# Four state-space layers on one core: the lines layer's table of slots is rearranged

## The chip, the cores and the metric

The kernel runs on one core of a Trainium2 chip. Its time is the device time of one execution in microseconds (us); the median of three runs is 17365.62 us (17365.36 to 17379.11). The engines are TensorE (PE: matrix products), VectorE (DVE), ScalarE (ACT), GpSimd (POOL) and SyncE (SP), which here only issues DMA transfers. Each works through its own queue of instructions in order and waits on semaphores for the others.

## What is computed

Eight images of 48 x 48 pixels and 96 channels go through four layers, each with a group norm before it and a residual addition behind it. Layers 0 and 3 are two-dimensional selective scans over 2304 positions, layer 1 is a filtered two-layer perceptron, and layer 2, the "lines" layer, scans every row and every column of 48 pixels in both senses. Its core, for one direction:

```python
xz = x @ in_w
xi, z = jnp.split(xz, 2, axis=-1)
xi = jax.nn.silu(causal_conv4(xi) + conv_b)
dt_low, Bm, Cm = jnp.split(xi @ xproj_w, [6, 22], axis=-1)
dt = jax.nn.softplus(dt_low @ dt_w + dt_b)
h = exp(dt * A) * h + dt * xi * Bm        # 192 channels x 16 states, along the line
y = (sum(h * Cm) + D * xi) * jax.nn.silu(z) @ outp_w
```

The four directions are then projected with `out_w`, summed and added to x.

## The kernel before, in words

**Layers.** `ss2d` runs layers 0 and 3, `lines` runs layer 2. Layer 1 has no stage of its own: its work items ("guests", class `Guest`) are slipped in between the work of layer 0 and of the lines layer. A guest item is a few matmuls into a PSUM bank that is free at that moment, and in the next slot an ACT instruction that takes the result out (`settle`).

**Blocks, turns, slots.** `scans` is shared by all three scan layers. The work is cut into images (8), directions (4) and blocks of 10 rows, 480 columns (the fifth block of a direction has 8 rows, 384 columns): 160 blocks a layer. A block has 8 slots, one for each pair of channel half and group of four states (`ORDER`), and two slots make a turn; so turn 0 holds slots 0 and 1, turn 3 slots 6 and 7. A slot has three units of [128 x columns], a turn six, which three scan instructions on DVE (L335) take two by two. I number the scans of a block 0 to 11.

**What one turn needs.** For every unit, ACT makes exp(dt * A) into one of two PSUM tiles `da` (L327, two instructions for each scan, so exp of scan n+2 can start when scan n has ended). The product of step size, input and B, called `dbu`, is made a turn ahead (L303), by DVE or POOL as the table `ON_POOL_L2` says: {slot: units of three that POOL makes}. DVE takes B from PSUM, where ACT copies it first (`copy_b`, L284, one bank; slots 3 and 4 have the same B and share a copy); a slot that POOL makes whole has no copy. After a scan, POOL multiplies by C (`make_hc`, L341, three units), and PE sums the states (`reduce`, L361 and L363).

**Order within a turn t** (end of `scans`), which is the order of every queue: scan 3t; POOL's C product for the slot before; `dbu` of the next turn's first slot on DVE; exp; both `dbu` of the next turn on POOL; scan 3t+1; exp; copy of B and `dbu` of the next turn's second slot on DVE; PE's sums; then the `aside` of the even slot; POOL's C product; exp for the next turn; scan 3t+2; copy of B; the gate product (L935) in turns 0 and 2; and the `aside` of the odd slot.

**`aside(at)`** (L405 to L425) settles the guest of the slot before, issues the loads due in this slot (B and C by `LOAD_BC`, the step sizes by `LOAD_DD`), runs the preparation steps (`stage1`) of the blocks to come, then the project and add steps of the block behind (`done`), and lets in a guest. The preparation of a block starts two blocks early; steps numbered 8 to 10 fall into slots 0 to 2 of the block before it:

```python
return {3: conv(0), 4: conv(1), 6: s2s3, 7: s5, 8: s6, 9: s7, 10: s8}
```

`conv` is four matmuls (L870) into the bank "sb" or "sa"; `s2s3` a Silu on ACT (L879) and a matmul (L889, bank "sa"); `s5` copies the result out (L894) and starts the step-size matmuls (L900); `s6` is Softplus on ACT (L907); `s7` the z matmuls (L913), the product dt * xi on POOL (L503) and the stores of the step sizes to DRAM (`store_dd`, L489); `s8` the Silu of z (L922). Silu, Softplus and exp need different function tables on ACT, so each of these steps brings two table loads. The stored step sizes are loaded back, spread over the partitions, by `load_dd` (L256), half 0 and half 1 of the block apart, into three rotating buffers. `project` (L944, bank "sa") and `add` (L950 or L952, DVE, `x += result`) follow a finished block. Banks open to guests by slot:

```python
guest.banks = lambda slot, clear: {0: ["sa"], 2: ["sb"], 3: ["sa"], 6: ["sb"]}.get(slot, [])
```

`guest.rate = 0.42` adds credit each slot, and an item costs 1.0.

Of the kernel before, what the change touches and what calls it, by code (L numbers as in the profile page):

```python
# [29 lines left out]
NG = 8  # L30
ORDER = [(0, sg) for sg in range(4)] + [(1, sg) for sg in range(3, -1, -1)]
LOAD_BC = (1, 1, 6, 7)
LOAD_DD = (3, 5)
NBUF = 7
UP = 96
UG = 73
# [8 lines left out]
CH = 96  # L45

ON_POOL_SS = {2: 1, 3: 3, 5: 1, 6: 1, 7: 3}
ON_POOL_L2 = {3: 2, 5: 3, 6: 1, 7: 3}


DIRS_SS = [(False, False), (True, False), (False, True), (True, True)]
# [10 lines left out]
def rows(t, n):  # L62

    return t[:, :n].rearrange("p (r s) -> p r s", s=SEG)
# [37 lines left out]
def vss_stack_kernel(ctx: ExitStack, tc: tile.TileContext, i: dict, out: bass.AP):  # L102
# [120 lines left out]
    def scans(dirs, order, restart, on_pool, a, pools, ps, stage1, opening, done, side, tail, ahead=None, guest=None):  # L223
# [9 lines left out]


        ahead = ahead or iter(())
        blocks = [Block(job, k, blk, n == 0, n == len(BLKS) - 1, dirs[k][1])
                  for job in range(nb) for k in order
                  for n, blk in enumerate(range(len(BLKS))[::-1 if dirs[k][1] else 1])]
# [14 lines left out]
        def load_dd(b, half):  # L253

            t = pools["dd"].tile([P, 3 * 2 * WMAX], F32, tag="dd", name="dd")
            nc.sync.dma_start(t[:, :6 * b.m], b.dd[half].unsqueeze(1).to_broadcast([32, 4, 6 * b.m]))  # L256
            b.got[half] = t[:, :6 * b.m].rearrange("p (g t m) -> p g t m", g=3, t=2)

        def load_bc(t):

            b, slot = blocks[t // NG], t % NG
            sg = ORDER[slot][1]
            other = t - slot + NG - 1 - slot
            n = min(free, key=lambda n: free[n])
            free[n] = other
            r = bufs[n]
            rows4 = b.bcd[8 * sg:8 * sg + 8, :].rearrange("(s w) n -> s (w n)", w=2)
            nc.sync.dma_start(r[:, LEAD:LEAD + 2 * b.n], rows4.unsqueeze(0).to_broadcast([32, 4, 2 * b.n]))

            lo, hi = LEAD - b.at.start, LEAD + b.n  # L270
            bcs[t] = bcs[other] = r[:, lo:hi + b.at.start], r[:, hi:hi + b.n]
# [105 lines left out]
        def run(t):  # L377
            for step in steps.pop(t, []):
                step()
# [25 lines left out]
        def aside(at):  # L405

            nblk, slot = at // NG + 1, at % NG
            if guest:
                guest.settle()
            if nblk < len(blocks):  # L410
                for n, of in enumerate(LOAD_BC):
                    if of == slot:
                        load_bc(NG * nblk + n)
                if slot in LOAD_DD:
                    load_dd(blocks[nblk], LOAD_DD.index(slot))
            clear = next(beside, True)
            run(at)
            for step in later.pop(at, []):
                step()
            while tail:  # L420
                tail.pop(0)()
            if guest:
                guest.turn(slot, clear)

        for t, (b, q) in enumerate(turns):  # L425
            at, nblk = 2 * t, t // (NG // 2)
# [64 lines left out]
    def sizes(b, half):  # L491

        return [b.dds[:, half, n, b.at] for n in range(2)]

    def make_room(b, pools):
        b.room = pools["dds"].tile([DH, LEAD + 4 * WMAX], F32, tag="dds", name="dds")
        b.dds = b.room[:, LEAD:LEAD + 4 * b.m].rearrange("p (h t m) -> p h t m", h=2, t=2)
# [279 lines left out]
    def lines(xin, xout, guest):  # L777
# [22 lines left out]
        def shift(t, dy, dx):  # L800

            at = (pad + dy) * step + pad + dx
            return t[:, at:at + H * step].rearrange("p (h w) -> p h w", w=step)[:, :, :W]
# [52 lines left out]
        def stage1(b):  # L856
            n = b.n
            col, rev = dirs[b.k]
            got = {}

            def shifted(off):
                return shift(colwise if col else rowwise, 0, off)[:, b.r0:b.r0 + b.nr, :]

            def conv(half):
                def run():
                    got["u", half] = ps("sa" if half else "sb", 1)
                    for tap in range(4):
                        off = tap - 3 if not rev else 3 - tap
                        at = ((b.k * 4 + tap) * 2 + half) * DH
                        nc.tensor.matmul(got["u", half][:, :n], lhsT=wide("cw", at),  # L870
                                         rhs=shifted(off), start=(tap == 0), stop=(tap == 3))
                return run

            def s2():
                b.uball = ubs[(len(BLKS) * (NK * b.job + b.k) + (len(BLKS) - 1 - b.blk if rev else b.blk)) % 3]
                b.uball = b.uball.rearrange("p (h n) -> p h n", h=2)
                b.ub = b.uball[:DH]
                for half in range(2):
                    nc.scalar.activation(b.ub[:, half, :n], got["u", half][:DH, :n], AF.Silu,  # L879
                                         bias=w["l2_cb"][:, b.k, half:half + 1])  # L880

            def s2s3():
                s2()
                s3()

            def s3():
                got["p"] = ps("sa", 1)
                for half in range(2):
                    nc.tensor.matmul(got["p"][:, :n], lhsT=wide("xp", (2 * b.k + half) * NBC), rhs=b.uball[:, half, :n],  # L889
                                     start=(half == 0), stop=(half == 1))  # L890

            def s4():
                b.bcl = pools["bcl"]
                nc.scalar.copy(b.bcl[:NBC, :n], got["p"][:NBC, :n])  # L894

            def s5():
                s4()
                for half in range(2):
                    got[half] = ps("sb" if half else "sa", 1)
                    nc.tensor.matmul(got[half][:, :n], lhsT=wide("dtw", (2 * b.k + half) * DH), rhs=b.bcl[:, :n],  # L900
                                     start=True, stop=True)

            def s6():
                nc.sync.dma_start(b.bcd, b.bcl[:2 * NS, :n])
                make_room(b, pools)
                for half in range(2):
                    nc.scalar.activation(sizes(b, half)[0], got[half][:DH, :n], AF.Softplus,  # L907
                                         bias=w["l2_dtb"][:, b.k, half:half + 1])

            def s7():  # L910
                for half in range(2):
                    got["z", half] = ps("sb" if half else "sa", 1)
                    nc.tensor.matmul(got["z", half][:, :n], lhsT=wide("inz", (2 * b.k + half) * DH),  # L913
                                     rhs=shifted(0), start=True, stop=True)
                make_du(b, b.ub[:, :, :n].rearrange("p h (r s) -> p h r s", s=SEG))
                for half in range(2):
                    store_dd(b, half)

            def s8():
                b.zb = up.tile([DH, 2, BMAX], F32, tag="zb", name="zb")  # L920
                for half in range(2):
                    nc.scalar.activation(b.zb[:, half, :n], got["z", half][:DH, :n], AF.Silu)  # L922

            return {3: conv(0), 4: conv(1), 6: s2s3, 7: s5, 8: s6, 9: s7, 10: s8}

        def opening(b, half):
            return wide("diag", (2 * b.k + half) * DH), b.uball[:, half, :b.n]
# [3 lines left out]
        def done(b, half, y):  # L931
            n = b.n
            if half == 0:
                gated[b] = gp.tile([DH, 2, BMAX], F32, tag="gated", name="gated")
            nc.vector.tensor_mul(gated[b][:, half, :n], b.zb[:, half, :n], y[:DH, :n])  # L935
            if half == 0:
                return []
            got = {}

            def project():  # L940
                got["o"] = ps("sa", 1)
                t = gated.pop(b)
                for h in range(2):
                    nc.tensor.matmul(got["o"][:, :n], lhsT=wide("wo", (2 * b.k + h) * C, DH), rhs=t[:, h, :n], start=(h == 0), stop=(h == 1))  # L944

            def add():
                xv = seq(xs[b.job], dirs[b.k][0])[:, b.r0:b.r0 + b.nr, :]
                v = rows(got["o"][:C], n)
                if b.k == 0:
                    nc.vector.scalar_tensor_tensor(xv, v, w["l2_outb"], xv, ALU.add, ALU.add)  # L950
                else:
                    nc.vector.tensor_add(xv, xv, v)  # L952
                if b.k == NK - 1 and b.last:
                    nc.sync.dma_start(xout[b.job], xs[b.job])

            return [(1, project), (2, add)]

        def side(job):
            used = NG
# [21 lines left out]
                yield from front(job + 1, tail.append, wait())  # L981

        dirs = DIRS_L2
        guest.banks = lambda slot, clear: {0: ["sa"], 2: ["sb"], 3: ["sa"], 6: ["sb"]}.get(slot, [])
        guest.psum = lambda tag: ps(tag, 1)
        guest.rate = 0.42
        scans(dirs, range(NK), True, ON_POOL_L2, a, pools, ps, stage1, opening, done, side, tail, guest=guest)
        stack.close()

# [264 lines left out]
    guest = Guest(stack, x1, x2)  # L1254
# [98 lines left out]
```

## Time and profile before

| what | value |
|---|---|
| profiled execution, time / span | 17373.84 us / 17371.9 us |
| median of the runs | 17365.62 us |
| lines layer, first dbu to last add | 5899 to 11833 us |
| its images 1 to 7, from output to output | 759, 737, 761, 742, 736, 724, 704 us |
| busy over the whole span | PE 76%, DVE 91%, ACT 80%, POOL 88% |
| last guest result stored | 10045 us |
| granted TensorE clock | 0.843 |

A page of the profile gives busy time by engine and by group of instructions (line, engine, operation, tile written from tiles read, shape), with the idle time ahead of a group and what ended it. The list of waits gives for each pair of waiting group and releaser the total in us, the number of times and the longest. A timeline row is: start in us, duration in us, engine, line, operation, tiles, shape, how many instructions are merged in it, and in brackets the idle time before it with its releaser. The window rows give for a stretch its length and then, for PE, PEld (weight loads), DVE, ACT and POOL, the busy us and the number of instructions, then the granted clock, DMA share and GB/s.

### The profile page before, as it was taken

The numbers are of one execution on the slowest core, as the hardware profiler recorded it, in microseconds if no ns is written. First come the engines' busy times: TensorE is split into PE (matmuls) and PEld (weight loads), VectorE is DVE, ScalarE is ACT, GpSimd is POOL, SyncE is SP. The second block draws the span as 40 slices with busy tenths as digits, with TensorE's granted clock in tenths as the row PEclk, the third lists the DMA queues.
The fourth block names the chain that finished last, engine by engine and source line by source line (L and its number), as shares of the span: only waits on it lengthen the run. The fifth ranks groups of instructions, "written<-read, shape, count | busy, mean of one in ns | idle before, by whom it ended". The sixth has DMA issues, their size and how long they took to land.

```text
span 17371.9 us, 169003 instructions
## 1 busy us (share of the span) xinstructions
PE 13193.7 (76%) x53740; PEld 4744.7 (27%) x53740; DVE 15807.2 (91%) x9840; ACT 13897.8 (80%) x20972; POOL 15212.7 (88%) x8159
## 2 busy tenths in 40 slices
PE   6778788878787677777777777776777777777776
PEld 1223232323232333233233322221222222222221
DVE  7999999998899789899889999996999999999998
ACT  6888888878787688888888888886878878878876
POOL 7998888988889788888888888887999999999998
PEclk7888888888897888899889988887878878878877
DMA  4555555454545344444444444443455555555454
GB/s 141 178 174 169 176 168 179 167 183 165 173 169 181 130 149 165 149 157 154 156 155 149 159 158 155 150 155 128 171 173 176 174 174 175 174 169 179 169 176 144
DMA packets 887919, 2843.67 MB, mean 164 GB/s; under 512 B 353468, under 2 KB 421788, under 8 KB 760206
## 3 DMA queue, kind: packets, MB, share of 16 engines
q1 hardware_dynamic: 887022, 2832.85, 48.0%
q8 instruction: 423, 6.93, 0.2%
q14 instruction: 474, 3.88, 0.1%
HBM read 2384.40 MB, written 448.17 MB: 163 GB/s over the span
## 4 chain that ended last, share of the span: by engine, by line
ACT 22%; DVE 21%; POOL 19%; issue 14%; PE 13%; DMA 10%; SPq 1%; POOLq 0%; DVEq 0%; ACTq 0%
DVE dbu L335 14%; POOL dbu L341 12%; ACT ps_da L327 8%; DVE dbu L303 6%; POOL dbu L303 4%; DMA dd<-dds 4%; DMA dd<-dd 3%; ACT L327 3%; PE ps_y L361 2%; POOL dds L503 2%; ACT ps_b L284 1%; PE ps_sa L944 1%; PE ps_sa L889 1%; DMA bc<-bcd 1%; ACT L907 1%
## 5 line engine op out<-in xcount | busy, mean ns | idle before, releaser
L335 DVE TENSOR_TENSOR_SCAN dbu<-ps_da,dbu 128x968 f32<-128x968 f32 (+3 forms) x5760 | 11823.5, 2075 | 814.5 <-ACT ps_da L327 653.1
L341 POOL TENSOR_TENSOR dbu<-dbu,bc 128x1440 f32<-128x1440 f32 (+1 forms) x3840 | 10069.9, 2635 | 1775.7 <-DVE dbu L335 1715.3
L327 ACT ACTIVATE ps_da<-dd,w_l_a 128x484 f32<-128x484 f32 (+3 forms) x11520 | 7423.0, 649 | 2308.3 <-DVE dbu L335 2078.8
L361 PE MATMUL ps_y<-dbu,w_red 128*32 128x480 f32 (+1 forms) x23040 | 4206.5, 651 | 1588.0 <-POOL dbu L341 1554.0
L363 PE MATMUL ps_y<-dbu,w_red 128*32 128x480 f32 (+1 forms) x7680 | 4168.0, 651 | 0.0
L303 DVE TENSOR_TENSOR dbu<-dd,ps_b 128x962 f32<-128x962 f32 (+5 forms) x2880 | 3831.0, 1330 | 286.1 <-ACT ps_b L284 157.3
L303 POOL TENSOR_TENSOR dbu<-dd,bc 128x481 f32<-128x481 f32 (+5 forms) x2240 | 3913.5, 1762 | 22.5 <-DMA dd<-dd 18.2
L361 PEld LDWEIGHTS ps_y<-dbu,w_red 128*32 128x32 f32 x23040 | 724.9, 118 | 5000.1 <-POOL dbu L341 3338.6
L284 ACT COPY ps_b<-bc 128x482 f32<-128x482 f32 (+3 forms) x2720 | 1448.8, 533 | 227.1 <-DVE dbu L303 185.3
L578 PE MATMUL ps_side<-xpad,w_l_cw 128*128 128x480 f32 (+1 forms) x2880 | 1360.4, 611 | 46.4 <-ACT g_room L1179 16.3
L327 ACT ACT_TABLE_LOAD x993 | 1274.0, 1283 | 17.5
L707 PE MATMUL ps_s<-bcl,square 128*128 128x480 f32 (+1 forms) x1280 | 890.0, 786 | 324.1 <-ACT dds L711 169.5
L357 PE MATMUL ps_y<-big,eye 128*128 128x480 f32 (+1 forms) x960 | 745.0, 865 | 243.5 <-ACT big L758 238.9
L717 PE MATMUL ps_s<-big,square 128*128 128x480 f32 (+1 forms) x1280 | 844.9, 790 | 66.1 <-ACT g_room L1179 18.4
L503 POOL TENSOR_TENSOR dds<-dds,big 96x960 f32<-96x960 f32 (+1 forms) x320 | 706.7, 2209 | 144.9 <-ACT dds L735 144.6
L578 PEld LDWEIGHTS ps_side<-xpad,w_l_cw 128*128 128x128 f32 x2880 | 575.0, 210 | 815.0 <-issue 703.4
L889 PE MATMUL ps_sa<-ub,square 128*128 128x480 f32 (+1 forms) x640 | 411.7, 782 | 394.2 <-ACT ub L879 394.2
L363 PEld LDWEIGHTS ps_y<-dbu,w_red 128*32 128x32 f32 x7680 | 661.9, 118 | 0.0
L870 PE MATMUL ps_sb<-xpad,square 128*128 128x480 f32 (+1 forms) x1280 | 595.2, 611 | 84.7 <-ACT g_room L1179 32.7
L870 PE MATMUL ps_sa<-xpad,square 128*128 128x480 f32 (+1 forms) x1280 | 537.9, 561 | 0.0
L711 ACT ACTIVATE dds<-ps_s,w_l_dtb 96x480 f32<-96x480 f32 (+1 forms) x640 | 405.1, 633 | 124.6 <-DMA dd<-dds 82.9
L758 ACT COPY big<-ps_y 96x480 f32<-96x480 f32 (+1 forms) x640 | 471.6, 737 | 38.7 <-PE ps_y L363 37.4
(244 smaller groups left out, 12498.7 us busy)
## 6 DMA issues: line engine op xcount, KB each, us to landing
dd<-dd SPq DMA_DIRECT2D x512, 1452.0 KB
bc<-bcd SPq DMA_DIRECT2D x1536, 480.0 KB
dd<-dd SPq DMA_DIRECT2D x256, 1440.0 KB
dd<-dds SPq DMA_DIRECT2D x512, 363.0 KB
dd<-dd SPq DMA_DIRECT2D x128, 1164.0 KB
bc<-bcd SPq DMA_DIRECT2D x384, 384.0 KB
dd<-dds SPq DMA_DIRECT2D x256, 360.0 KB
dd<-dd SPq DMA_DIRECT2D x64, 1152.0 KB
```

Of the source, the lines that this page charges most:

```text
L284: nc.scalar.copy(bps[t][:, :bcs[t][0].shape[1]], bcs[t][0])
L303: engine.tensor_mul(o, du, by.unsqueeze(1).to_broadcast([P, hi - lo, by.shape[1]]))
L327: nc.scalar.activation(da[:, at:at + b.m], b.got[half][:, u % 3, 0, :], AF.Exp, scale=a[:, b.k, ci:ci + 1])
L335: nc.vector.tensor_tensor_scan(db, da, db, 0.0, ALU.mult, ALU.add)
L341: nc.gpsimd.tensor_mul(h, h, bcs.pop(2 * t + sub)[1].unsqueeze(1).to_broadcast([P, 3, n]))
L361: nc.tensor.matmul(y[32 * g:32 * g + 32, :n], lhsT=wc["red"][:, :32], rhs=hc[:, g, b.at], start=False, stop=(slot == 3))
L363: nc.tensor.matmul(y[DH:, :n], lhsT=wc["red"][:, 32:], rhs=hc[:, 2, b.at], start=False, stop=(slot == 3))
L503: nc.gpsimd.tensor_mul(du, dt, u)
L578: nc.tensor.matmul(pu[:, :n], lhsT=flat[:, at:at + P], rhs=xpad[:, r0 + dy:r0 + dy + nr, dx:dx + W], start=(tap == 0), stop=(tap == 8))
L707: nc.tensor.matmul(got["p"][:, :n], lhsT=wide("dtw", (2 * b.k + half) * DH), rhs=b.bcl[:, :n], start=True, stop=True)
L717: nc.tensor.matmul(got["p"][:, :n], lhsT=wide("xp", (2 * b.k + half) * NBC), rhs=uall[:, half], start=(half == 0), stop=(half == 1))
L870: nc.tensor.matmul(got["u", half][:, :n], lhsT=wide("cw", at), rhs=shifted(off), start=(tap == 0), stop=(tap == 3))
```

## The change

Only tables and slots of the lines layer change. The addition to x moves from two to three slots behind the finished block (slot 3 to slot 4); the two convolutions from slots 3 and 4 to 4 and 5; the load of step-size half 0 from slot 3 to slot 2; POOL makes `dbu` of slots 4, 6 and 7 whole, instead of two units of slot 3, slot 5 whole, one unit of slot 6 and slot 7 whole (nine units either way); and guests may enter in slots 0, 3 and 6 instead of 0, 2, 3 and 6. Layers 0 and 3 keep their tables.

```diff
-LOAD_DD = (3, 5)
+LOAD_DD_SS = (3, 5)
+LOAD_DD_L2 = (2, 5)
...
-ON_POOL_L2 = {3: 2, 5: 3, 6: 1, 7: 3}
+ON_POOL_L2 = {4: 3, 6: 3, 7: 3}
...
+        load_in = LOAD_DD_L2 if restart else LOAD_DD_SS
...
-                if slot in LOAD_DD:
-                    load_dd(blocks[nblk], LOAD_DD.index(slot))
+                if slot in load_in:
+                    load_dd(blocks[nblk], load_in.index(slot))
...
-            return {3: conv(0), 4: conv(1), 6: s2s3, 7: s5, 8: s6, 9: s7, 10: s8}
+            return {4: conv(0), 5: conv(1), 6: s2s3, 7: s5, 8: s6, 9: s7, 10: s8}
...
-            return [(1, project), (2, add)]
+            return [(1, project), (3, add)]
...
-        guest.banks = lambda slot, clear: {0: ["sa"], 2: ["sb"], 3: ["sa"], 6: ["sb"]}.get(slot, [])
+        guest.banks = lambda slot, clear: {0: ["sa"], 3: ["sb"], 6: ["sb"]}.get(slot, [])
```

## The prediction, made before the changed kernel ran

> **What bounds the kernel now.** Only the lines layer is touched, so I read the window rows of that stage first, then its list of waits, then one block as a timeline.
>
> ```profile
> 5900.00:11800.00 5900.00, 4506.11 (x18182) 1721.81 (x18182) 5345.67 (x3421) 4883.50 (x7125) 4893.75 (x2267) 0.87 0.44 154
> ```
>
> The third busy figure is DVE's: 5345.67 of 5900 us, 91%; ACT and POOL stand at 83%. DVE bounds the stage, and a change can win at most its 554 us of idle time. The waits say what ends it:
>
> ```profile
> DVE dbu L335 <- ACT ps_da L327: 275.0, 252, 3.3
> ...
> DVE x L952 <- PE ps_sa L944: 128.7, 105, 3.2
> ...
> DVE dbu L303 <- DMA dd<-dd: 93.8, 48, 34.3
> ...
> DVE x L950 <- PE ps_sa L944: 45.3, 35, 2.6
> ...
> SPq L256 <- DMA dd<-dds: 1696.6, 295, 9.0
> ```
>
> Numbering the scans of each block along DVE's timeline puts these waits in place. Scan 3 (the first of turn 1) waits for its exp in 158 of 160 blocks, 191 us; the add waits for its projection 141 times, 175 us; the first dbu of the next block, in turn 3, waits for step sizes 47 times, 59 us (the 34 us one is the start of the layer); scans 0 and 1 wait 28 and 38 us. The last row is on SP: the load of the step sizes waits for their own store. One block, DVE first:
>
> ```profile
> 8996.45 2.16 DVE L335 TENSOR_TENSOR_SCAN dbu<-ps_da,dbu 128x960 f32<-128x960 f32 x1 [1.64 <-ACT ps_da L327]
> 8998.52 1.63 DVE L303 TENSOR_TENSOR dbu<-dd,ps_b 128x1440 f32<-128x1440 f32 x1
> 9000.07 4.20 DVE L335 TENSOR_TENSOR_SCAN dbu<-ps_da,dbu 128x960 f32<-128x960 f32 x2
> 9004.87 0.71 DVE L950 SCALAR_TENSOR_TENSOR x<-ps_sa,w_l_outb,x 96x480 f32<-96x480 f32 x1 [0.60 <-PE ps_sa L944]
> ```
>
> ```profile
> 8998.64 1.36 ACT L327 ACTIVATE ps_da<-dd,w_l_a 128x480 f32<-128x480 f32 x2 [0.49 <-DVE dbu L335]
> 9000.02 1.28 ACT L922 ACT_TABLE_LOAD   x1
> ...
> 9002.36 1.28 ACT L327 ACT_TABLE_LOAD   x1
> 9003.65 1.36 ACT L327 ACTIVATE ps_da<-dd,w_l_a 128x480 f32<-128x480 f32 x2
> ```
>
> ```profile
> 8996.52 1.56 SPq L489 DMA_DIRECT2D dd<-dds  x2
> 9006.98 5.22 SPq L256 DMA_DIRECT2D dd<-dd  x2
> ```
>
> See two things. Scan 5 ends at 9004.27, but the exp for scan 6 ends at 9005.01: the add's wait covers ACT being 0.74 us late behind the Silu of z. And the load of step sizes leaves 10 us after the store; the dbu that needs it came at 9015.66 after a wait of 0.24, so it took 8.7 us.
>
> **POOL's units.** By shape, DVE makes 3, 2 and 1 units in 1630, 1126 and 628 ns, POOL 3, 2 and 1 in 2738, 1887 and 1036. DVE's block was 4 x 1630 + 1126 + 628 = 8274 ns, and becomes 5 x 1630 = 8150: 19 us less over the blocks. The weight is in where they go.
>
> Turn 0 gains: dbu of slot 3 is three units instead of one on DVE, 1.0 us more work (0.8 in short blocks) ahead of scan 3, which waits there for ACT in any case. Taking from each block's wait the smaller of wait and 1.0 gives 129 us over the 156 blocks whose rows I could follow.
>
> Turn 1 loses: dbu of slot 5 comes to DVE, so its copy of B (L284, 540 ns) now stands ahead of the Silu of z on ACT; before, slot 5 had no copy, and that of slot 6 stood behind the exp. There are five copies either way.
>
> Turn 2 puts slots 6 and 7 whole on POOL, two operations of 2.74 us in a row between C products. From the end of scan 1 POOL then has nine of 2.74 and the dt * xi product with its memset (2.02) up to the C product of slot 5, 26.6 us, and PE's sums behind it take 1.7. Scan 3 starts about 4.3 us after scan 1's end, so PE is free 24.0 us into turn 1. Behind those sums on PE stands L889, which ACT's Silu releases at 9.0 (to scan 6, next part) + 7.6 (turn 2: three scans, add, gate) + 7.0 (scan 9, dbu, copy, table load, two Silu) = 23.6. PE would be 0.4 us late; in the block above, where scan 3 waited long, not at all. The result goes by L894 to the exp of scan 1. In the 108 blocks with guests half have under 0.35 us of slack there; block by block a slip of 0.2, 0.4 or 1.0 us costs 8, 19 or 61 us. The 47 blocks without guests have 1 us of slack: nothing. I take 0.3 us, 13 us; it cannot gain, since PE waits for the Silu now. The dbu themselves are in time: slot 4 at 6, slots 6 and 7 at 14 and 17 us into turn 1, wanted at 9.0, 16.6 and 20.2.
>
> **Add and convolutions.** The projection stays in slot 2, so an add two scans later finds it done: 171 us of wait go (156 blocks). What is late next is the exp of scan 6. From the end of scan 3, ACT takes 6.40 us in the block above, plus 0.54 for the copy, 6.94; DVE has two scans and a dbu, 5.66. So 1.28 us of waiting in long blocks, and since ACT was 1.4 us late in short ones, 1.9 there: over all blocks 242 us, where add and scan 6 waited 177. This part costs 65 us. The add's own 0.7 to 0.9 us only moves. From below: were the copy hidden, this place would gain 17. The convolutions (2.85 us each) move behind the sums of turn 1 on PE; bank "sb" is settled in slot 4 ahead of the first, "sa" read by the add ahead of the second, and slot 6 reads them 4 us later. PE was idle 2.5 us ahead of L889 per block, so I count nothing beyond the slip above.
>
> **Step sizes.** In the queue order of the changed program the load moves past at most a guest transfer. In 124 of 156 blocks nothing stood between store and load, and it still left 9.6 us after the store: SP waits for the store, not for the slot. The two blocks where three or four guest transfers came between (16 us) and the others with such a neighbour waited about 16 us above the rest; from 0 to 16, I take 10.
>
> But the round trip is a loop: store to load 9.6, load to dbu 8.7, then 17.7 to the next store (four scans, three dbu, the C product and the dt * xi product). 36.0 us a block, beside a mean long block of 37.5. Whatever is won between store and dbu is only kept where the step sizes have landed. Sum so far: 129 - 65 + 19 = 83 us, 0.53 a block. In 46 blocks DVE already waits there, so all is lost; elsewhere the spare time (dbu less load less 8.65, 7.4 in short blocks) is under 0.43 us in a quarter of the long ones. Cutting each block's gain at its spare time leaves 51 us.
>
> Here the Trainium skill differs ("DMA: Bandwidth & Descriptors", section "Anatomy of one DMA — SWDGE (gpsimd) path"): about 2.0 us plus bytes over 436 GB/s. It is stated for another issuing engine; for the 360 KB store it would be 2.8 us, an estimate. Then loads would leave 6.8 us sooner, the loop would not bind, and the 83 would stand. The row has 9.6 us in nearly every block, so I take 51.
>
> **Guests.** At three places a block instead of 3.36 by credit, the last result is stored, by the order of SP's queue, about 12 blocks later. Long blocks with guests last 38.0 us, without 36.4. If an item costs, nothing changes; if a block with guests costs, 12 x 1.6 = 19 us. I take 12. One guest fewer between z and the convolutions frees PE, not DVE.
>
> **Sum.** 51 + 10 - 13 - 12 = 36 us off the profiled 17373.8. That execution is 8.2 us above the median of the runs, so the time is 17365.6 - 36 = 17330.
>
> **The rivals.** *Exchange without gain*, 20%: the loop of step sizes takes all; landing 1 us later than 8.65, as with bc loads and guests beside it in a dozen blocks, eats another 35, and 17360 is left. For it: the 1696 us of SP waits; against it: half of the blocks have 1 us to spare. That moving the load does nothing is in both.
>
> *POOL's row of four*, slower, 19%: in turn 2 the C products come so late that PE starts L889 1.5 us late, and `s5`, the exp and scan 1 follow in all guest blocks: 61 + 108 x 0.5 = 115 us, against 51 + 10 - 12 = 49 of other gain: 66 us slower, 17432; at 1.2 us (83) still 34 slower, 17400. It decides from a slip of about 0.85 us, where the 49 are gone. For it: POOL has no pause from scan 1 to there; against it: the count of its work gives 0.4.
>
> *More*, 20%: the copy of B falls into a pause of ACT and transfers land sooner once the order is quieter: without the copy the sum is 164 before the loop's cut and 82 after it, 92 with the ordering: 17274, and 17250 if the cut is a quarter smaller.
>
> *As summed*, 41%, own range 17305 to 17352.
>
> **Numbers.** About 0.2% (35 us) is what a measurement can tell from no change. Faster by more: the 20% and two thirds of 41%, 0.47; within: the rest and the exchange, 0.34; slower 0.19. For 8 in 10 the range goes from 17250 to 17405.
>
> **What would show it.** Right: the add's waits nearly gone; scan 3 waiting 0.2 to 0.4 us a block instead of 1.2; scan 6 waiting 1.3 to 1.9 us for ACT, about 240 us in all; dbu on step sizes above 59 us; store to load still 9.6. Wrong: scan 6 not waiting, scan 1 waiting over 100 us, or the load leaving sooner after its store.

## The result, and the profile after

Changed kernel: 17276.92 us, median of six runs (17266.99 to 17280.5); before, six runs, 17368.66. The ratio is 0.9944 (0.9931 to 0.9957): 92 us or 0.5% faster. The direction was forecast, the size was 36. The profiled execution has a span of 17274.2 us (17371.9 before), so the sums below are made against 97.7. The lines layer's images 1 to 7 now take 740, 728, 733, 727, 732, 723 and 699 us; the last guest is stored at 10395 instead of 10045 us; the granted clock over the span is 0.849.

The window row of the lines stage, after (stretch and length, then busy us of PE, PEld, DVE, ACT, POOL, then granted clock, DMA share, GB/s):

```profile
5900.00:11700.00 5800.00, 4406.68 (x18177) 1666.92 (x18177) 5333.69 (x3261) 4882.12 (x7124) 4868.65 (x2107) 0.89 0.45 157
```

DVE still bounds the stage: 5333.69 of 5800 us, 92%. Its list of waits, after:

```profile
DVE dbu L337 <- ACT ps_da L329: 347.2, 301, 3.3
DVE dbu L305 <- DMA dd<-dd: 113.4, 72, 35.1
```

Waits for `ps_sa` by the add have left the list but for one of 1.9 us; scans waiting for exp grew from 275 to 347 us, and `dbu` waiting for step sizes from 94 to 113 (35 of each is the start of the layer). SP's row for the load that waits for its store says that this round trip has not become shorter:

```profile
SPq L258 <- DMA dd<-dds: 1763.7, 314, 8.9
```

One block on DVE, after:

```profile
9068.22 1.65 DVE L305 TENSOR_TENSOR dbu<-dd,ps_b 128x1440 f32<-128x1440 f32 x1
9069.79 2.15 DVE L337 TENSOR_TENSOR_SCAN dbu<-ps_da,dbu 128x960 f32<-128x960 f32 x1
9073.25 4.20 DVE L337 TENSOR_TENSOR_SCAN dbu<-ps_da,dbu 128x960 f32<-128x960 f32 x2 [1.30 <-ACT ps_da L329]
9077.36 0.53 DVE L954 TENSOR_TENSOR x<-x,ps_sa 96x384 f32<-96x384 f32 x1
...
9085.89 1.65 DVE L305 TENSOR_TENSOR dbu<-dd,ps_b 128x1440 f32<-128x1440 f32 x1 [3.19 <-DMA dd<-dd]
```

And ACT in the same block:

```profile
9067.59 0.54 ACT L286 COPY ps_b<-bc 128x480 f32<-128x480 f32 x1
9068.15 1.28 ACT L924 ACT_TABLE_LOAD   x1
9069.44 0.57 ACT L924 ACTIVATE zb<-ps_sa 96x480 f32<-96x480 f32 x1
...
9070.49 1.28 ACT L329 ACT_TABLE_LOAD   x1
9071.78 2.64 ACT L329 ACTIVATE ps_da<-dd,w_l_a 128x480 f32<-128x480 f32 x4
```

The add no longer waits, but the copy of B stands ahead of the Silu of z, and scan 6 (9073.25) waits 1.30 us for the exp behind that chain. This is the exchange that the prediction described (1.28 us there). The 3.19 us at 9085.89 is the loop of step sizes; SP's rows of the same block show the store at 9067.05 and the load 9.60 us later:

```profile
9067.05 1.56 SPq L491 DMA_DIRECT2D dd<-dds  x2
9076.65 0.56 SPq L258 DMA_DIRECT2D dd<-dd  x1
```

The table has DVE's waits in the lines layer by place, in us, counted along DVE's timeline and scaled to 160 blocks. "dd" is `dbu` waiting for step sizes; "rest" is scans 0, 4 and 7, `dbu` waiting for the copy of B, and what rounding leaves. The last two columns are outside DVE. "ACT" is ACT's wait for PE ahead of the `bcl` copy (L894, later L896), the settling of a guest directly in front of it included, scaled in the same way. "L889" is the mean in ns of that matmul (L891 after), from the groups of PE between 6000 and 9900 us.

| kernel | time | add | dd | gate | s1 | s3 | s6 | rest | total | ACT | L889 |
|---|---|---|---|---|---|---|---|---|---|---|---|
| before | 17368.66 | 179 | 61 | 20 | 39 | 191 | 6 | 41 | 537 | 95 | 737 |
| after | 17276.92 | 0 | 79 | 0 | 11 | 60 | 225 | 73 | 448 | 42 | 614 |
| e1_pool_only | 17370.04 | 156 | 115 | 35 | 46 | 69 | 24 | 80 | 525 | 104 | 748 |
| e2_all_but_pool | 17321.56 | 0 | 48 | 2 | 16 | 199 | 169 | 43 | 477 | 65 | 702 |
| e3_load_only | 17369.88 | 161 | 58 | 26 | 32 | 193 | 8 | 44 | 522 | 87 | 740 |
| e7_four | 17356.22 | 0 | 77 | 6 | 31 | 63 | 224 | 103 | 504 | 70 | 683 |
| e8_three_guests | 17393.0 | 146 | 57 | 10 | 68 | 212 | 9 | 51 | 553 | 157 | 869 |
| e9_four_pool_old | 17378.18 | 0 | 40 | 10 | 50 | 202 | 169 | 62 | 533 | 103 | 764 |
| e10_again | 17362.98 | 172 | 54 | 27 | 20 | 188 | 9 | 46 | 516 | 68 | 593 |
| e11_three_again | 17319.55 | 177 | 67 | 0 | 11 | 177 | 10 | 46 | 488 | 41 | 608 |
| e12_two_not_three | 17365.35 | 0 | 63 | 2 | 45 | 72 | 225 | 114 | 521 | 94 | 773 |
| e4_slot5 | 17274.58 | 0 | 131 | 1 | 14 | 59 | 172 | 56 | 433 | 49 | 643 |
| e5_store | 17175.83 | 0 | 0 | 0 | 8 | 52 | 225 | 64 | 349 | 40 | 587 |
| e6_both | 17102.63 | 0 | 0 | 2 | 16 | 58 | 170 | 47 | 293 | 58 | 593 |

The first two rows close the account: 537 - 448 = 89 us of waits, and DVE's busy time went from 15807.2 to 15796.7, 10.5 more; 99.5 together against a span shorter by 97.7. (The account is of one execution; for the other runs it leaves up to some 25 us unexplained.) What was not forecast stands in the gate and s1 columns: 20 and 28 us of waits for PE and ACT that went. PE made the same matmuls, but L889 in 614 instead of 737 ns, and its pause ahead of them shrank. The group's row (busy us and mean ns, then PE's idle time ahead of it) before:

```profile
L889 PE MATMUL ps_sa<-ub,square 128*128 128x480 f32 (+1 forms) x416 | 250.6, 737 | 251.6 <-ACT ub L879 251.6
```

and after:

```profile
L891 PE MATMUL ps_sa<-ub,square 128*128 128x480 f32 (+1 forms) x428 | 208.8, 614 | 79.8 <-ACT ub L881 79.6
```

### The profile page after: what moved, and what is told of

It is laid out like the page before. It is cut to its first block, busy times and chain, and to the rows that moved or that the text cites. A ratio compares the mean times of both kernels' runs of the same rounds, so it can differ in the third digit from the quotient of the medians.

```text
span 17274.2 us, 168621 instructions
## 1 busy us (share of the span) xinstructions
PE 13082.7 (76%) x53740; PEld 4691.8 (27%) x53740; DVE 15796.7 (91%) x9680; ACT 13897.4 (80%) x20972; POOL 15188.2 (88%) x7999
## 4 chain that ended last, share of the span: by engine, by line
ACT 22%; POOL 21%; DVE 19%; issue 15%; DMA 13%; PE 9%; SPq 1%; POOLq 0%; DVEq 0%; ACTq 0%
POOL dbu L343 13%; DVE dbu L337 12%; ACT ps_da L329 8%; DMA dd<-dds 6%; DVE dbu L305 6%; POOL dbu L305 5%; DMA dd<-dd 4%; ACT L329 3%; POOL dds L505 3%; PE ps_y L363 2%; ACT ps_b L286 2%; DMA bc<-bcd 1%; PE ps_side L580 1%; ACT L737 1%; PE ps_s L709 1%
## 5 line engine op out<-in xcount | busy, mean ns | idle before, releaser
L363 PE MATMUL ps_y<-dbu,w_red 128*32 128x480 f32 (+1 forms) x23040 | 4261.4, 656 | 1676.9 <-POOL dbu L343 1643.4
L365 PE MATMUL ps_y<-dbu,w_red 128*32 128x480 f32 (+1 forms) x7680 | 4222.1, 656 | 0.0
L305 POOL TENSOR_TENSOR dbu<-dd,bc 128x481 f32<-128x481 f32 (+3 forms) x2080 | 3883.8, 1883 | 4.2 <-DMA bc<-bcd 4.1
L872 PE MATMUL ps_sa<-xpad,square 128*128 128x480 f32 (+1 forms) x1280 | 521.2, 548 | 0.0
L915 PE MATMUL ps_sa<-xpad,square 128*128 128x480 f32 (+1 forms) x320 | 243.5, 854 | 322.8 <-ACT g_room L1181 108.9
```

The lines of the kernel that those rows point to most:

```text
L305: engine.tensor_mul(o, du, by.unsqueeze(1).to_broadcast([P, hi - lo, by.shape[1]]))
L363: nc.tensor.matmul(y[32 * g:32 * g + 32, :n], lhsT=wc["red"][:, :32], rhs=hc[:, g, b.at], start=False, stop=(slot == 3))
L365: nc.tensor.matmul(y[DH:, :n], lhsT=wc["red"][:, 32:], rhs=hc[:, 2, b.at], start=False, stop=(slot == 3))
```

## The experiments

The first theory was that POOL's new units brought the surplus: nine operations in a row would hold PE's sums back until just before L889, so that PE no longer paused. The rival gave it to the convolutions a slot later and to the guests. A third, made after the first nine runs, was about what PE does just ahead of L889. The times of before on the chips of these runs were 17369.95 to 17376.03; ratios are against those.

### e1_pool_only: before with POOL's units alone

```diff
-ON_POOL_L2 = {3: 2, 5: 3, 6: 1, 7: 3}
+ON_POOL_L2 = {4: 3, 6: 3, 7: 3}
```

> The kernel before with POOL's new units (slots 4, 6, 7) and nothing else. Theory A (POOL's row of four delays PE's sums until just ahead of the Silu, so PE does not pause ahead of L889 and runs it and the guest behind it faster): the pause ahead of L889 falls from 2.3 us to under 1 us a block, scan 1 waits under 15 us in all instead of 37, scan 3 about 60 us instead of 180; add and scan 6 together wait about 240 us instead of 177. 17300 to 17335 us. Theory B (scan 1 and the gate product gained from the convolutions and guests, that is from PE's order): scan 1 still waits 35 to 55 us and the gate 19 us, and the time is 17335 to 17360 us.

Measured: 17370.04, ratio 0.9995 (0.9986 to 1.0004): no difference that can be told. Scan 3 waits 122 us less (129 were counted), but step sizes cost 54 more, the gate 15, scan 6 18, scans 1, 4 and 7 another 40, and L889 stays at 748 ns, though the pause right ahead of it fell from 251.6 to 139.6 us. The first theory falls: POOL's row of four does not make L889 faster, and its units are worth nothing by themselves that can be measured.

### e2_all_but_pool: all of the change except POOL's units

```diff
-ON_POOL_L2 = {4: 3, 6: 3, 7: 3}
+ON_POOL_L2 = {3: 2, 5: 3, 6: 1, 7: 3}
```

> The changed kernel with POOL's old units (slots 3, 5, 6, 7): addition, convolutions, load and guests moved, nothing else. Theory A: the pause ahead of L889 stays over 1.5 us, scan 1 waits 30 to 45 us, scan 3 about 180 us, the add no more, and scan 6 about 160 us in its place: 17335 to 17360 us. Theory B: scan 1 under 15 us, gate product near 0, 17290 to 17325 us.

Measured: 17321.56, 0.9971 (0.9958 to 0.9984): 54 us faster than before. Scan 1's wait falls to 16 and the gate's to 2 with POOL's units as they were, so these two gains come from the other parts. POOL's units are worth some 40 us on top of them (45 by the times, 38 by the ratios) and 6 without. The two parts give 60 us apart and 92 together, but the intervals are about 20 us each way, so these runs alone do not show that the parts help each other.

### e3_load_only: before with the load of step sizes a slot sooner

```diff
-                if slot in LOAD_DD:
-                    load_dd(blocks[nblk], LOAD_DD.index(slot))
+                load_in = (2, 5) if restart else LOAD_DD
+                if slot in load_in:
+                    load_dd(blocks[nblk], load_in.index(slot))
```

> The kernel before with only the load of step-size half 0 in slot 2. By the sum of the prediction the load leaves 9.6 us after its store as before and 0 to 16 us are won: 17350 to 17368 us. If the slot set the load, the 57 us of waiting for step sizes would go: about 17310 us.

Measured: 17369.88, 0.9994 (0.9985 to 1.0004). `dbu` waits 58 us for step sizes instead of 61, and store to load still takes 9.64 us (median). The earlier issue is worth nothing that can be measured, but the interval reaches from 7 us slower to 26 faster, so it cannot tell 0 from the 10 us that were forecast.

### e7_four: after with four places for guests

```diff
-        guest.banks = lambda slot, clear: {0: ["sa"], 3: ["sb"], 6: ["sb"]}.get(slot, [])
+        guest.banks = lambda slot, clear: {0: ["sa"], 2: ["sb"], 3: ["sb"], 6: ["sb"]}.get(slot, [])
```

> The changed kernel with guests let into four places again (slot 2 as well as 0, 3, 6; bank sb in slots 2, 3 and 6). If the smaller number of guests a block is what freed scan 1, its wait goes back from 10 to over 30 us and the time rises by 25 to 40 us, to 17300 to 17317 us. If not, scan 1 stays at 10 to 15 us and the time stays within 15 us of the changed kernel's 17277 us.

Measured: 17356.22, 79 us slower than after, more than expected. Scan 7 waits 42 us where it waited for nothing (the cause is shown under e12), scan 1 31, and L889 takes 683 ns. Guests matter, and more than by their number: the last guest of the changed kernel comes only 350 us later than before, some nine blocks.

### e8_three_guests: before with three places for guests

```diff
-        guest.banks = lambda slot, clear: {0: ["sa"], 2: ["sb"], 3: ["sa"], 6: ["sb"]}.get(slot, [])
+        guest.banks = lambda slot, clear: {0: ["sa"], 3: ["sa"], 6: ["sb"]}.get(slot, [])
```

> The kernel before with the guest place in slot 2 closed (slots 0, 3 and 6 left) and nothing else. If the fewer places are what won the 54 us of the run without POOL's table, scan 1 waits under 20 us instead of 39 and the time is 17305 to 17335 us. If it needs the convolutions and the addition a slot later, under 15 us are won: 17355 to 17375 us.

Measured: 17393.0, 1.001 (1.0 to 1.0019): 21 us slower, where less guest work a block was to help or do nothing. L889 takes 869 ns, ACT waits 157 us in front of the `bcl` copy and scan 1 waits 68.

### e9_four_pool_old: convolutions, add and load later, four guests, POOL's old units

```diff
-ON_POOL_L2 = {4: 3, 6: 3, 7: 3}
+ON_POOL_L2 = {3: 2, 5: 3, 6: 1, 7: 3}
...
-        guest.banks = lambda slot, clear: {0: ["sa"], 3: ["sb"], 6: ["sb"]}.get(slot, [])
+        guest.banks = lambda slot, clear: {0: ["sa"], 2: ["sb"], 3: ["sb"], 6: ["sb"]}.get(slot, [])
```

> The changed kernel with POOL's old units and guests in four places (slot 2 as well, bank sb in slots 2, 3 and 6): addition, convolutions and load moved alone. If the later convolutions are what frees scan 1 and the gate product, these wait about 16 and 2 us as with three guest places, and the time is 17310 to 17340 us. If the guest in slot 2 takes ACT right behind the late exp of scan 6, scan 7 waits 40 us, scan 1 over 30, and the time is 17370 to 17405 us.

Measured: 17378.18, 1.0002 (0.9993 to 1.0012), no gain; scan 7 waits 22 us. With e8 this leaves the rival in pieces too: neither the later convolutions nor the missing guest gives anything alone, together (e2) they give 54 us. In e2 the first convolution follows the guest of slot 3 in the same bank and has to wait until ACT has taken that guest out (48 us in the groups of PE, 9 in e9), so PE works on convolutions until nearer to L889: the pause ahead of it is 194.6 us in e2 and 249.3 in e9. The third theory is that this is what counts: what PE did just before L889 sets how fast L889 and the guest behind it run. It makes a strange forecast, that *more* work for PE at this place makes the kernel faster.

### e10_again and e11_three_again: the second convolution twice

`e10` is before, `e11` is e8, each with the second convolution's four products made once more in slot 5 into the same tile, so the result is the same and PE works more.

```diff
-            def conv(half):
+            def conv(half, again=False):
                 def run():
-                    got["u", half] = ps("sa" if half else "sb", 1)
+                    if not again:
+                        got["u", half] = ps("sa" if half else "sb", 1)
...
-            return {3: conv(0), 4: conv(1), 6: s2s3, 7: s5, 8: s6, 9: s7, 10: s8}
+            return {3: conv(0), 4: conv(1), 5: conv(1, True), 6: s2s3, 7: s5, 8: s6, 9: s7, 10: s8}
```

> The kernel before with the second convolution's four matmuls issued once more in slot 5, into the same bank with the same operands: the result is unchanged, PE has 2.9 us more work a block, lying after slot 4 and ahead of L889. Theory C (PE's pause ahead of L889 sets how fast it runs L889 and the guest behind it, and so scan 1's wait): the pause falls from 2.5 us to under 1.5, L889 from 737 ns to 620 to 690, scan 1 waits under 25 us instead of 39, and the time falls by 10 to 30 us, to 17340 to 17360, though work was added. Theory D (the number of guests and their copies on ACT): L889 may quicken, but scan 1 waits as long or longer and the time is the same or up to 40 us more.

> The kernel before with guest places 0, 3 and 6 and the repeated convolution in slot 5. Without the repetition it had the longest pause, L889 at 869 ns and scan 1 waiting 68 us, 17393 us. Theory C: L889 under 700 ns, scan 1 under 30 us, 17340 to 17365 us. Theory D: scan 1 stays over 50 us, 17390 to 17430 us.

Measured: e11 takes 17319.55, 0.9971 (0.9961 to 0.9981), 73 us less than e8, which does less. The row of L889 in the groups of PE for e8:

```profile
L889 PE MATMUL ps_sa<-ub,square 128*128 128x480 f32 (+1 forms) x416 | 301.3, 869 | 284.0 <-ACT ub L879 284.0
```

and for e11:

```profile
L890 PE MATMUL ps_sa<-ub,square 128*128 128x480 f32 (+1 forms) x424 | 204.7, 608 | 112.5 <-ACT ub L880 112.3
```

The same instruction takes 608 instead of 869 ns, and PE's pause ahead of it is less than half as long. But a pause of one length can go either way. The second convolution and L889 on PE in one block of e8:

```profile
9090.91 3.49 PE L870 MATMUL ps_sa<-xpad,square 128*128 128x480 f32 x8
...
9098.73 3.40 PE L889 MATMUL ps_sa<-ub,square 128*128 128x480 f32 x4 [2.25 <-ACT ub L879]
```

and of e11:

```profile
9069.05 6.71 PE L871 MATMUL ps_sa<-xpad,square 128*128 128x480 f32 x16
...
9080.34 1.88 PE L890 MATMUL ps_sa<-ub,square 128*128 128x480 f32 x4 [2.51 <-ACT ub L880]
```

Pauses of 2.25 and 2.51 us stand ahead of them, yet four matmuls take 3.40 us in e8 and 1.88 in e11. The window rows say why. The granted clock (the figure before the last two) is read here in stretches of 3.41 us, the grid on which all its changes in this layer lie. In e8:

```profile
9092.11:9095.53 3.42, 3.42 (x16) 1.41 (x18) 3.42 (x4) 2.40 (x5) 3.01 (x2) 1.00 0.91 315
9095.53:9098.94 3.41, 1.16 (x13) 0.34 (x6) 3.41 (x4) 3.32 (x6) 1.55 (x1) 1.00 0.69 273
9098.94:9102.35 3.41, 3.41 (x6) 1.08 (x6) 2.41 (x2) 2.60 (x4) 2.65 (x2) 0.50 0.00 0
```

and in e11:

```profile
9075.18:9078.59 3.41, 2.65 (x20) 0.79 (x18) 3.07 (x2) 1.98 (x4) 0.00 (x0) 1.00 0.97 365
9078.59:9082.00 3.41, 1.66 (x4) 0.87 (x5) 3.41 (x5) 3.37 (x5) 2.23 (x1) 1.00 0.43 168
```

PE was busy all through the stretch before in e8 too. What differs is that its pause lies within one stretch, in which PE is busy 1.16 of 3.41 us, 34%; the next is granted half the clock, and nearly all of L889 falls into it. In e11 the pause is spread over two, 78% and 49% busy, and the clock stays up. Over the whole lines layer of e8, of the stretches at full clock all 194 with PE busy under 40% were followed by one at half, and 14 of 951 with PE busy over 50%. So the idle time within a stretch counts, right ahead of L889 or not. PE's mean busy share in the 3.41 us before L889 orders the runs nearly as the time of L889 does; among them e8 0.21 (869 ns), before 0.30 (737), e12 0.39 (773), e1 0.40 (748), e2 0.45 (702), after 0.67 (614), e11 0.68 (608), e10 0.88 (593).

The Trainium skill ("TensorE: Matmul & The Clock Gate", section "Part 1: The HAM clock gate") has the kind of this: PE runs at half rate after an idle window of about 3.4 us and at full rate again after as long under load, in windows that run freely. The trace agrees in the length of the windows and in the two rates (0.50 and 1.00). By the page no clock would have been lost in these two blocks, since neither pause fills a window; the measurement decides, and here a window with PE busy for a third of it was enough.

The way to DVE is in the groups of ACT. For the guests of slot 6 (bank "sb"), e8:

```profile
L1179 ACT ACTIVATE g_room<-ps_sb,g_b 128x365 f32<-128x365 f32 (+1 forms) x33 | 18.3, 556 | 30.2 <-PE ps_sb L1177 30.2
```

and e11:

```profile
L1180 ACT ACTIVATE g_room<-ps_sb,g_b 128x365 f32<-128x365 f32 (+1 forms) x35 | 19.3, 551 | 3.0 <-PE ps_sb L1178 2.9
```

In slot 7 ACT settles the guest that PE made behind L889, and only then copies `bcl` and goes on to the exp. It waited 0.9 us for each guest of this kind in e8 (30.2 us for 33) and 0.1 in e11. Over the layer ACT's wait at this place fell from 157 to 41 us, and scan 1's from 68 to 11.

In the order of before the same repetition is worth little: e10 takes 17362.98, 0.9994 (0.9984 to 1.0003). L889 goes to 593 ns, ACT's wait to 68 and scan 1's to 20, but the gate waits 7 us more. A faster L889 is not enough by itself.

### e12_two_not_three: after, the guest of slot 3 moved to slot 2

```diff
-        guest.banks = lambda slot, clear: {0: ["sa"], 3: ["sb"], 6: ["sb"]}.get(slot, [])
+        guest.banks = lambda slot, clear: {0: ["sa"], 2: ["sb"], 6: ["sb"]}.get(slot, [])
```

> The changed kernel with guest places 0, 2 and 6 instead of 0, 3 and 6: still three, but the first convolution no longer waits in slot 4 for the copy of a guest from slot 3. Theory C: the convolutions start sooner, the pause ahead of L889 grows from 0.8 to over 1.2 us, L889 from 614 to 670 ns or more, scan 1 from 11 to 25 us or more, and the time is 17295 to 17340 us. If three guests a block are what counts, within 15 us of 17277. If the guest of slot 2 is what costs, because its copy stands on ACT behind the late exp of scan 6: scan 7 waits about 40 us and scan 1 stays near 11.

Measured: 17365.35, 0.9997 (0.9987 to 1.0006): 88 us slower than after, with as many guests. L889 goes from 614 to 773 ns, ACT's wait from 42 to 94, scan 1's from 11 to 45, and scan 7, which did not wait, waits 49 us. So moving one guest costs nearly the whole gain, but in two parts. One is the third theory's: the first convolution, ahead of which PE stood idle 81 us in the groups of after until ACT had taken the guest out of the bank, now waits for nothing there and is done earlier. (That wait alone is not enough for a fast L889: before had 78 us of it, with the convolutions a slot sooner.) The other is scan 7, which did not wait in before either. Its cause is seen on ACT:

```profile
9135.89 1.36 ACT L329 ACTIVATE ps_da<-dd,w_l_a 128x480 f32<-128x480 f32 x2
9138.64 0.40 ACT L1192 COPY g_room<-ps_sb 73x288 f32<-73x288 f32 x1 [1.39 <-PE ps_sb L1190]
9138.93 2.64 ACT L329 ACTIVATE ps_da<-dd,w_l_a 128x480 f32<-128x480 f32 x4
```

and on DVE:

```profile
9140.33 2.16 DVE L337 TENSOR_TENSOR_SCAN dbu<-ps_da,dbu 128x960 f32<-128x960 f32 x1 [0.82 <-ACT ps_da L329]
```

A guest of slot 2 is settled between the exp of scan 6, which is late already, and the exp of scan 7. The settling waits for the guest's matmuls, 1.39 us here, and the exp waits behind it; this is so in 48 of the 57 blocks where scan 7 waits. How the 88 us divide between the two parts is read from the waits (34 at scan 1, 49 at scan 7), not tested apart.

### e4_slot5: after, with one copy of B less

POOL makes slot 5 whole instead of slot 4. Slot 4 then shares the copy of slot 3, and none stands ahead of the Silu of z.

```diff
-ON_POOL_L2 = {4: 3, 6: 3, 7: 3}
+ON_POOL_L2 = {5: 3, 6: 3, 7: 3}
```

> The changed kernel with slot 5 on POOL instead of slot 4 (units in slots 5, 6, 7). Slot 4 on DVE shares the copy of B with slot 3, so turn 1 has no copy ahead of the Silu of z and a block has four copies instead of five. If the copy costs what the prediction priced (0.54 us a block in turn 1), scan 4, dbu of turn 1 and scan 6 together wait about 165 us instead of 253, the wait for step sizes takes part of that back (75 to about 110 us), and 30 to 55 us are won on the changed kernel: 17222 to 17247 us. If the copy was hidden, the time is within 15 us of 17277.

Measured: 17274.58, 2 us under after, where a gain was expected. Scan 6 waits 53 us less and scan 4 19 less, but `dbu` waits 52 more for step sizes: the loop through DRAM took most of it.

### e5_store: after, with the store of step sizes in three pieces

```diff
-        nc.sync.dma_start(b.dd[half].rearrange("j (g m) -> g j m", g=3), b.dds[:, half].rearrange("p t m -> p (t m)"))
+        for g in range(3):
+            nc.sync.dma_start(b.dd[half][:, 2 * g * b.m:2 * (g + 1) * b.m], b.dds[32 * g:32 * g + 32, half].rearrange("p t m -> p (t m)"))
```

(in the lines layer only)

> The changed kernel, in the lines layer each store of step sizes split into three transfers of 32 partitions (six issues instead of two). If the store is what the load waits for, store to load falls from 9.6 us to 4 to 6 us, DVE's wait for step sizes from 75 to under 15 us, and 40 to 70 us are won: 17207 to 17237 us. If the step sizes only cover other waits, their wait goes but scans 0, 1 and 3 wait more, and the time stays within 15 us of 17277. If the six issues hold up SP, loads of B and C come late and it is slower.

Measured: 17175.83, 0.989 (0.9874 to 0.9907), 101 us under after, more than expected. SP in one block:

```profile
9007.24 2.64 SPq L495 DMA_DIRECT2D dd<-dds  x6
9010.22 0.52 SPq L258 DMA_DIRECT2D dd<-dd  x1
```

The load leaves 2.98 us after the first store instead of 9.60. What is left of the waits for step sizes is the start of the layer:

```profile
DVE dbu L305 <- DMA dd<-dd: 29.5, 1, 29.5
```

The bytes are the same. The outermost dimension of a transfer went from 3 to 32, and its number from one to three for each half. The Trainium skill ("DMA: Bandwidth & Descriptors", section "Rules for kernel authors") says that an outermost dimension of fewer than 16 confines a transfer to so many of the engines. The trace shows that it is this and not the number of transfers. While the two stores of a block ran in the changed kernel, the DMA share (the figure before the last) was 0.18, about 3 of 16 engines, for both together:

```profile
9068.00:9076.00 8.00, 5.61 (x32) 1.58 (x30) 6.70 (x5) 6.87 (x10) 8.00 (x4) 0.91 0.18 55
```

and it was 0.88 in e5:

```profile
9008.00:9010.00 2.00, 2.00 (x10) 0.23 (x12) 2.00 (x2) 1.97 (x4) 2.00 (x2) 0.51 0.88 238
```

Among the packets of the trace, each store of after closes with three of 4 bytes, and the load leaves just behind the third (9076.25 and 9076.65 us); in e5 the six transfers close with 96, 16 each. So the 9.6 us were the price of three engines, which the prediction did not weigh; cut, the store comes near the 2.8 us of its estimate.

### e6_both: e4 and e5 together

> The two before together: slot 5 on POOL instead of slot 4, and the store of step sizes in three. If the loop of step sizes is what eats part of each gain, the two add up and more: 17277 minus 88 for the copy, minus 60 to 75 for the loop, 17115 to 17150 us. If they cover each other, no better than the better of the two alone.

Measured: 17102.63, 0.9847 (0.9833 to 0.9862): 1.5% under before, 174 us under after, and a little better than expected. The copy of B that was worth 2 us under the loop is worth 73 without it.

## Why the prediction came out right in sign and short in size

**POOL's units, turn 0.** Right: 129 us were to leave scan 3's wait; 131 left. The work saved on DVE, 19 us by the rows, shows as 10.5.

**Add and convolutions.** Right in kind: 65 us were to be lost as scan 6 takes the place of the add. Add and scan 6, the two places that the prediction counted, went from 185 to 225 us, 40 more, with scan 6 at 225 for 242 predicted. Another 30 went to scan 4 and to `dbu` waiting for the copy of B, which it did not count; that the two make 70 is in part luck.

**Step sizes.** The loop binds, as the prediction said: its wait rose to 79, the store still took 9.6 us, and e5 shows that it binds in 101 us of time. It cost 18 us of added waits, where the prediction cut 32. The 10 us for the order of loads are neither borne out nor excluded (e3). The weighing against the page's price was decided rightly for this kernel, but the reason for the 9.6 us was not seen: the store's outermost dimension of 3.

**The step that failed: the slip at L889.** The prediction has "I take 0.3 us, 13 us; it cannot gain, since PE waits for the Silu now." It counted when L889 starts and took its duration, and that of the guest behind it, for fixed. The chain from the Silu to scan 1 got shorter instead: L889 737 to 614 ns, ACT's wait ahead of the `bcl` copy 95 to 42 us, scan 1 39 to 11, and the gate's wait 20 to 0. That is 48 us gained where 13 were to be lost, a swing of 61 us. The gain was 56 us larger than forecast (92 against 36); the smaller terms (the work saved, the loads, the guests, the loop) about cancel. Shown is that PE's work ahead of L889 changes L889's speed, scan 1 and the time (e11 against e8), that this goes by the granted clock, that in this order of slots the place of the guest is needed for it (e12: scan 1 back from 11 to 45 us), and that POOL's units alone do not bring it (e1). Argued only is the gate's part, which fell with the rest in e2 and e11, stayed at 2 in e12, and was not tried alone.

**Guests.** 12 blocks at 1.6 us were to be lost. The last guest came some nine blocks later (350 us), and the dearer part of a guest proved to be its place: the median long block with guests went from 37.8 to 36.8 us, without from 36.7 to 36.4, so what a guest adds, 1.1 us by these medians where the prediction took 1.6, shrank to 0.4. In the old order one place fewer costs 21 us (e8).

**Rivals.** *POOL's row of four* did not happen: scan 1 waits less. *Exchange without gain* is what POOL's units alone do (e1). *More* came at its time, 17274, by luck: no copy fell into a pause and no transfer landed sooner, and its sum leaves out the 25 us for slip and guests that the main sum takes off. The range of *as summed*, 17305 to 17352, was missed; the wide one holds the result only because it reached down to *more*.

Two things stay open: why the repeated convolution helps e8 by 73 us and before by 9, though L889 is fast in both (21 of the 73 only win back what e8 had lost, and with three guest places the gate waits 0 us instead of 27; the rest was not tried), and 15 us of e12's loss and 23 of e7's that no wait of DVE in the table holds.

## What to carry to other kernels

Before a step is priced as "can only slip", look at how its duration spreads within one run: a matmul that takes 566 to 1170 ns at one shape (L889 at 480 columns) can gain as well as lose from what stands ahead of it. Where a round trip through DRAM is nearly as long as the block, gains elsewhere are hidden in it, so cut the loop first and judge the rest afterwards; here one copy was worth 2 us before the cut and 73 after. Parts of a change that give nothing alone, or lose (e9, e8), can give most of it together (e2), so take away from the whole as well as adding to the start.

## What the hardware showed that was not expected

Extra matmuls made the kernel 73 us faster (e11 against e8), in a kernel that PE does not bound. The clock of PE followed its busy share in fixed stretches of 3.41 us: after one that was 34% busy it was halved and four matmuls took 3.40 us, while a longer pause that fell across two stretches, 78% and 49% busy, left it up, and they took 1.88. A store with an outermost dimension of 3 ran at a DMA share of 0.18 and took 9.6 us until the load behind it could leave; in three pieces of 32 partitions, with four more transfers to issue, it ran at 0.88 and took 3.0.
